# Odd gelu blocks of layer 0 turned by transposing DMAs into a table of half rows; the expert bias as a product, outputs copied by ScalarE

## The chip, the core and the metric

The kernel runs on one core of one Trainium2 chip. A core has a matmul engine (TensorE; the profile splits it into PE, the products, and PEld, the loading of their stationary operand), VectorE (DVE), ScalarE (ACT), GpSimd (POOL) and SyncE (SP, which here only issues transfers), and 16 DMA engines that carry out transfers issued from the engines' queues. SBUF is the on-chip memory of 128 partitions, PSUM the memory that products are written to. The metric is the device time of one execution in microseconds; lower is better.

## The reference, cut to what matters

Two layers work on 128 graphs of 64 nodes, N = 8192 tokens of 256 numbers, all in f32. Each layer is a graph convolution followed by a mixture of experts. The change touches the mixture of layer 0 only:

```python
H = gelu(xf @ W1 + b1)                      # 8192 x 1024, the same for all experts
probs = softmax(H @ Wg + bg)                # 8 experts
assign = argmax(probs)
for e in range(8):
    y = H @ Wd[e] + bd[e]                   # 1024 -> 256
    out += where(assign == e, probs[:, e:e+1] * y, 0)
```

Here xf is the layer-normed output of the graph convolution. Every token needs the second product with one expert's Wd alone, so the kernel sorts the rows of H by expert and runs 128 rows of one expert at a time. Layer 1 (an attention over the same graphs, and a mixture gated by a graph of 1,048,576 edges) comes behind; its edge list is sorted into keys early, beside layer 0.

## The kernel before, in words

The program is written as Python generators ("streams") whose steps are interleaved, and a scheduler then sets each engine's order. Each engine runs its instructions in that order, and each engine's DMA issues stand in its queue with the waits that they carry.

**Parts, up to about 620 us.** The 64 tiles of 128 tokens form 16 groups g of GR = 4 tiles. Parts i = 0 to 9 each take two groups of two kinds of work: `graph(g)`, the graph convolution (parts 0 to 7, L626 to L690), and `gated(g)`, the mixture's first half (parts 2 to 9, two parts behind). Beside them run `factors` (the layer norms' factors), `look` (degrees; its copies L596 run on POOL), and `collect` (parts 1 to 7): this loads a chunk of edges on SP (`src`, `dst`, L279), finds the largest keys by repeated max and match_replace on DVE, and stores what is left over with SP (`left`, L316). In parts 8 and 9 a stream of counts runs in `collect`'s place (compares on DVE L203, products L341).

`gated(g)` works in this order:
- the four tiles normed by ACT (L734), turned by TensorE (L746), copied by ACT into `zT` (L747);
- `hidden` (L489 to L503): for each of NH = 8 blocks q of 128 hidden units, two products of 128x128 by 128x512 (L498) and a gelu on ACT into `hTs[q]` (L501), a tile with hidden units on partitions and the group's 512 tokens along it. The pool `bh` has 10 such buffers;
- `turned(q)` (L752 to L756) turns block q back: four TensorE transposes of f32 128x128 (L755) into a PSUM bank of `psb` (2 buffers, shared with L746), then an ACT copy (L756) into `rows`, one buffer of 128 x 4 x 1024. It follows BEHIND = 4 blocks behind `hidden`, the last four behind the gating steps;
- gate products (L765), logits turned (L774), softmax and argmax on DVE (L779 to L794), the rank of each token among its expert's by products with a triangular matrix (L802, L803), and from it the row `pos` in the sorted table (L806 to L814);
- four indirect DMAs issued by POOL (L818), each of which sends 128 rows of 4 KB to rows `pos` of the DRAM table `hrows`.

Transfers behind these on SP: zero fills of `hrows` (from L976) and of `yrows` (L983), and, after part 7, the load of all eight Wd into `wd` (L1010).

**Early tiles, about 620 to 664 us.** `early_slots` (L871 to L943) does 8 tiles that are known to be complete two parts before the end. Its row and expert numbers are loaded into SP's and PE's registers; each tile is loaded by two transfers (L900), turned (L911, L913), multiplied by its expert (L932), gets the bias from a broadcast load (L929) by a DVE add (L940), and is stored (L942). `slot_tables` (L1012) works out beside it which 128 rows of `hrows` each of the remaining slots takes, its expert and its output row.

**Slots, about 664 to 964 us.** `slots` (L1199 to L1277) runs 60 slots, one expert each:
- `load(t)` on SP two slots ahead: `hin`, 128 rows of 4 KB (L1238), from a row number in a register; every fourth slot loads registers for the next four;
- `turn(t)` one slot ahead: eight TensorE transposes (L1247) into two PSUM banks (`pst`, 4 buffers), two ACT copies into `hTt` (L1250);
- the bias of the slot's expert broadcast over 128 rows by SP (L1262), eight f32 products of 128x128 by 128x256 that add up in `py` (L1265; `psy`, 2 buffers), the DVE add into `y` (L1273), the store to `yrows` on SP (L1274).

Beside the slots run the counts of keys (DVE compares L203, products L341), the last steps of the key sort, and `back_first` (L1171 to L1202), which for finished tiles gathers rows of `yrows` by POOL (L1193), adds them to `x` on DVE (L1184) and takes statistics (L1185). From 964 us on layer 1 runs, which the change doesn't touch.

The order of steps in the slots loop, which decides what stands between two slots' products:

```python
for t in range(first, end):
    if t + 2 < end: load(t + 2)
    if t + 1 < end: turn(t + 1)
    ...                       # bias load, 8 products, add, store
    yield add_bd              # the count stream's products come here
```

## Time and profile before

| what | value |
|---|---|
| median of 11 runs | 1975.65 us (1972.37 to 1980.22) |
| the profiled execution | 1975.63 us; span 1973.9 us; granted clock 0.987 |
| PE / PEld / DVE / ACT / POOL busy | 94 / 67 / 69 / 48 / 23 % of the span |
| slots' products L1265 | 960 records, 217.1 us |
| slots' copies L1250 on ACT | 120, 64.3 us |
| transposes L755 in `gated` | 512, 62.3 us of weight loads |
| scatters L818 on POOL | 64, 64.6 us |

All times below are of the profiled execution. A group in the profile is one line of the kernel on one engine, with the tiles it writes and reads ("py<-wd,hTt"), its shape, the number of records, the busy time, the mean of one in ns, and the engine's idle time before them with what ended most of it. A table of stretches gives, for a window A:B in us, the window's length and the busy time of each engine in it, with the number of records, then the granted clock, the share of the 16 DMA engines in use and GB/s. Matmuls are pipelined and their ends are modelled, so a busy PE isn't PE at its peak. An f32 product stands as two records where it is 512 or 256 columns wide: the 480 products of the slots are 960 records.

### The profile page before, as it was taken

To read this page: it belongs to the slowest core of one execution; us is meant where nothing else is said; L and a number is where in the kernel's file an instruction comes from. 1 tells how busy PE (TensorE), PEld (TensorE's weight loads), DVE (VectorE), ACT (ScalarE), POOL (GpSimd) and SP (SyncE) were. 2 spreads that over 40 slices of the span, in tenths; PEclk is the share of its full clock that TensorE was granted. 3 is DMA by queue.
4 is the path that set the end of the run, shared out by engine and by line. 5 is a ranking of instruction groups with operands and counts; after the bars stand their busy time and mean duration, and the time that the engine had idled before them with its cause. 6 is when DMAs were issued, how large, how long until landed. Compare 5 with 4: busy or idle time off the path is not lost. (4 is left out here: it accounts for less than half of the span.)

```text
span 1973.9 us, 32697 instructions
## 1 busy us (share of the span) xinstructions
PE 1862.1 (94%) x10609; PEld 1323.8 (67%) x10609; DVE 1353.6 (69%) x4535; ACT 948.6 (48%) x1740; POOL 452.8 (23%) x467
## 2 busy tenths in 40 slices
PE   7888998989999999999978999999999989999999
PEld 5444545444556888888745666656676758888876
DVE  6789988873356899998498755857888543334435
ACT  4867667667664222122477676422434423334322
POOL 2010110101011011111141100015677643213223
PEclk9999999999999999999988999999999999999999
DMA  9752322323425555555314211473222359889833
GB/s 295 205 170 88 120 78 78 127 88 118 138 87 179 164 179 182 169 159 173 89 54 152 67 66 42 156 202 79 64 63 61 93 188 292 275 259 276 284 114 96
DMA packets 243552, 284.91 MB, mean 144 GB/s; under 512 B 55920, under 2 KB 195312, under 8 KB 243376
## 3 DMA queue, kind: packets, MB, share of 16 engines
q1 hardware_dynamic: 209392, 221.96, 36.3%
q0 software_dynamic: 23136, 60.48, 9.4%
q10 hardware_dynamic: 10848, 0.30, 0.3%
q8 instruction: 89, 1.46, 0.3%
q14 instruction: 87, 0.71, 0.1%
HBM read 159.40 MB, written 123.18 MB: 143 GB/s over the span
## 5 line engine op out<-in xcount | busy, mean ns | idle before, releaser
L498 PE MATMUL ph<-zT,w 128*128 128x512 f32 x512 | 247.9, 605 | 5.9 <-ACT zT L747 4.8
L1265 PE MATMUL py<-wd,hTt 128*128 x960 | 217.1, 379 | 0.9 <-ACT hTt L1250 0.9
L1265 PEld LDWEIGHTS py<-wd,hTt 128*128 128x128 f32 x960 | 177.8, 190 | 22.9 <-ACT hTt L1250 1.2
L1878 POOL DMA_INDIRECT got<-tsrc,esrc x144 | 156.5, 1087 | 156.6 <-DVE esrc L1849 77.5
L1250 ACT COPY hTt<-th 128x512 f32<-128x512 f32 x120 | 64.3, 589 | 238.5 <-PE th L1247 228.8
L1415 PE MATMUL py<-w,hT 128*128 128x256 f32 x736 | 172.3, 387 | 6.8 <-DVE td L2237 4.9
L1405 PE MATMUL ph<-zT,w 128*128 128x512 f32 x368 | 169.8, 604 | 0.0
L1415 PEld LDWEIGHTS py<-w,hT 128*128 128x128 f32 x736 | 138.1, 192 | 32.4 <-issue 8.8
L498 PEld LDWEIGHTS ph<-zT,w 128*128 128x128 f32 x512 | 91.8, 192 | 97.6 <-issue 78.8
L2363 ACT ACTIVATE hT<-ph,b1e 128x256 f32<-128x256 f32 x152 | 72.1, 474 | 176.9 <-PE ph L2359 100.5
L2359 PE MATMUL ph<-zTp,w1e 128*128 128x256 f32 x608 | 139.0, 382 | 3.9 <-DMA w1e<-in_L_ffn_W_dram 3.9
L1409 ACT ACTIVATE hT<-ph,b 128x512 f32<-128x512 f32 x92 | 63.1, 688 | 164.4 <-PE ph L1405 162.7
L818 POOL DMA_INDIRECT hrows<-rows,pos x64 | 64.6, 1009 | 337.2 <-issue 164.0
L2380 DVE TENSOR_TENSOR y<-py,b2e 128x256 f32<-128x256 f32 x76 | 32.3, 425 | 157.1 <-PE py L2372 147.0
L2372 PE MATMUL py<-w,hT 128*128 x608 | 137.5, 379 | 0.0
L2359 PEld LDWEIGHTS ph<-zTp,w1e 128*128 128x128 f32 x608 | 116.5, 192 | 20.3 <-issue 4.2
L501 ACT ACTIVATE hT<-ph,b 128x512 f32<-128x512 f32 x128 | 88.1, 688 | 80.8 <-PE ph L498 76.6
L660 PE MATMUL pre<-wd 128*128 128x512 f32 x256 | 124.1, 602 | 1.9 <-ACT wd L646 1.3
L2372 PEld LDWEIGHTS py<-w,hT 128*128 128x128 f32 x608 | 112.6, 190 | 13.8
L1405 PEld LDWEIGHTS ph<-zT,w 128*128 128x128 f32 x368 | 67.8, 191 | 68.0 <-issue 67.1
L2393 POOL DMA_INDIRECT back<-yslots,place x64 | 64.6, 1009 | 166.6 <-ACT yb L1431 49.0
L755 PEld LDWEIGHTS tz<-ident,hT 128*128 128x128 f32 x512 | 62.3, 143 | 54.5 <-issue 42.8
(499 smaller groups left out, 3872.3 us busy)
## 6 DMA issues: line engine op xcount, KB each, us to landing
hin<-hrows SPq DMA_DIRECT2D x60, 512.0 KB
w1e<-in_L_ffn_W_dram SPq DMA_DIRECT2D x38, 512.0 KB
yin<-ystore SPq DMA_DIRECT2D x24, 512.0 KB
yrows<-none SPq DMA_DIRECT2D x10, 1024.0 KB
zslots<-none SPq DMA_DIRECT2D x38, 256.0 KB
zin<-zslots SPq DMA_DIRECT2D x38, 256.0 KB
yslots<-y SPq DMA_DIRECT2D x76, 128.0 KB
ystore<-y SPq DMA_DIRECT2D x72, 128.0 KB
```

What stands on the lines that cost most here:

```text
L498: nc.tensor.matmul(ph, w1[:, c, q * P : q * P + P], zT[:, c, :], start=(c == 0), stop=(c == 1))
L501: gelus.append(S.activation(hT, ph, AF.Gelu, bias=b1[:, q : q + 1]).ins)
L660: nc.tensor.matmul(pre, xnT[:, c, n * P : n * P + P], wcat[:, c, :], start=(c == 0), stop=(c == 1),)
L818: nc.gpsimd.indirect_dma_start(hrows, bass.IndirectOffsetOnAxis(ap=pos[:, t : t + 1], axis=0), rows[:, k, :], None)
L1265: nc.tensor.matmul(py, hT[:, q, :], wd[:, bass.ds(e, 1), q, :].rearrange("p e f -> p (e f)"), start=(q == 0), stop=(q == NH - 1),)
L1405: nc.tensor.matmul(ph, w1[:, e, c, q * P : q * P + P], zT[:, c, :], start=(c == 0), stop=(c == 1))
L1415: nc.tensor.matmul(py, hTs[q][:, k * P : k * P + P], w2[:, e, q, :], start=(q == 0), stop=(q == NH1 - 1))
L1878: nc.gpsimd.indirect_dma_start(got, None, tsrc, bass.IndirectOffsetOnAxis(ap=esrc[:, b, at : at + 1], axis=0))
L2359: nc.tensor.matmul(ph, w1e[:, c, q * P : q * P + P], zT[:, c, :], start=(c == 0), stop=(c == 1))
L2363: pace[:] = [S, S.activation(hT, ph, AF.Gelu, bias=b1e[:, q : q + 1]).ins]
L2372: nc.tensor.matmul(py, hTs[q][:, k * P : k * P + P], w2[:, e, q, :].rearrange("p e f -> p (e f)"), start=(q == 0), stop=(q == NH1 - 1),)
L2393: nc.gpsimd.indirect_dma_start(got[n], None, yslots[h], bass.IndirectOffsetOnAxis(ap=place[h][:, j, t : t + 1], axis=0))
```

## The change

**Tables.** `hrows` gets half its width: 512 numbers, the even blocks q. The odd blocks go into a new DRAM table `halves` with two rows of 512 sixteen-bit words for each token. Both tables are zero-filled in part 1.

**`gated(g)`.** After the gelu of an odd block, SP issues a transposing DMA that reads `hTs[q]` as 128 x 1024 sixteen-bit words and writes eight 128x128 blocks of them turned into `half_rows` (128 x 8 x 512 words, one buffer): 256 KB each, 4 per group, 64 in all. `turned` is called for the even blocks alone, 4 times per group: behind gelu 3, 5 and 7 and behind the gate products. POOL's four scatters send rows of 2 KB instead of 4 KB, and eight more scatters per group send the rows of 1 KB of `half_rows` to `halves`. Their row numbers come from `p2`, two f32 products per group with `spread_pos`, two 0/1 matrices kept in buffers that are used later for `cnt`, `row_y`, `slot_e` and `slot_row`, and one DVE instruction that makes 2 * row + (0 or 1). The four columns of row positions that `p2` multiplies are those that DVE had copied to `pos` (the tile `m`).

**Early tiles.** Each loads one 256 KB tile from `hrows`, and a second by a transposing DMA from `halves`, which arrives turned; four TensorE transposes and one ACT copy per tile stay. The bias add stays on DVE.

**Slots.** `hin` is half as wide (256 KB); `hB` arrives turned by a transposing DMA from 256 rows of `halves`, issued by SP behind `hin`. Four transposes and one ACT copy stay of eight and two. The bias comes from a bf16 product of 128x96 by 96x256 ahead of the eight f32 products: each f32 bias is split into three bf16 pieces that add up to it exactly, and a 0/1 matrix picks the expert's. `bias_tables` builds both, in three steps ahead of `slot_tables`, in the region of `w1`. The broadcast load and the DVE add are gone; ACT copies `py` to `y` and stores it from its own queue. PE alone loads the expert's number, ACT the output row's. `psy` gets 3 buffers (2 before), `pst` 3 (4 before). The gathers of `back_first` are no longer declared apart from the stores.

The diff, cut to its core:

```diff
+hrows = dram.tile([E0 * N, FD // 2], F32, name="hrows")
+halves = dram.tile([E0 * N * 2, FD // 2], U16, name="halves")
 yrows = dram.tile([(NSLOT + EARLY) * P, D], F32, name="yrows")
 psel = const.tile([P, NT], F32, name="psel")
-row_y = const.tile([P, NT], I32, name="row_y")
 off = const.tile([P, NT, 64], U8, name="off")
-cnt = const.tile([P, NT], F32, name="cnt")
+sums = const.tile([P, 2 * NT], F32, name="cnt")
+cnt, row_y = sums[:, 0:NT], sums[:, NT:].bitcast(I32)
...
+    slot_at = w0.tile([P, 2 * NSLOT], F32, name="slot_e")
+    slot_e, slot_row = (slot_at[:, i : i + NSLOT].bitcast(I32) for i in (0, NSLOT))
+    spread_pos = sums, slot_at[:, 0:P]
+    for h, to in zip(HALVES, spread_pos):
+        V.tensor_copy(
+            to.rearrange("p (n e) -> p n e", e=2), ident[:, h].unsqueeze(2).to_broadcast([P, 64, 2])
+        )
...
+            of_row = bg1.tile([P, 2], I32, name="of_row")
+            nc.gpsimd.iota(of_row[:, 0:1], pattern=[[0, 1]], base=0, channel_multiplier=1)
+            V.tensor_scalar(of_row[:, 1:2], of_row[:, 0:1], 1, None, ALU.bitwise_and)
+            odd = of_row[:, 1:2].bitcast(F32)
+            V.tensor_copy(odd, of_row[:, 1:2])
+            of_row = of_row[:, 0:1]
...
-                rows = b2.tile([P, GR, FD], F32, name="rows")
+                rows = b2.tile([P, GR, FD // 2], F32, name="rows")
+                half_rows = b2.tile([P, 2 * GR, FD // 2], U16, name="half_rows")
 
                 def turned(q):
                     th = psb.tile([P, GR * P], F32, name="tz")
                     for k in range(GR):
                         nc.tensor.transpose(th[:, k * P : k * P + P], hTs[q][:, k * P : k * P + P], ident)
-                    S.copy(rows[:, :, q * P : q * P + P], th.rearrange("p (k n) -> p k n", k=GR))
+                    at = q // 2 * P
+                    S.copy(rows[:, :, at : at + P], th.rearrange("p (k n) -> p k n", k=GR))
 
                 for q, _ in enumerate(hidden(zT, hTs)):
-                    if q >= BEHIND:
-                        turned(q - BEHIND)
+                    if q % 2:
+                        at = q // 2 * P
+                        nc.sync.dma_start_transpose(half_rows[:, :, at : at + P], hTs[q].bitcast(U16))
+                        if q > 1:
+                            turned(q - 3)
...
-                turned(NH - BEHIND)
+                turned(NH - 2)
...
-                turned(NH - BEHIND + 1)
...
-                turned(NH - BEHIND + 2)
...
-                turned(NH - BEHIND + 3)
...
+                p2 = psg0.tile([P, GR * P], F32, name="ms")[:, 0 : 2 * GR].rearrange("p (k h) -> p k h", h=2)
+                for j in range(2):
+                    nc.tensor.matmul(p2[:, :, j], spread_pos[j], m, start=True, stop=True)
...
+                at = pr.rearrange("p k e -> p (k e)")[:, 0 : 2 * GR].bitcast(I32)
+                V.tensor_scalar(at, p2.rearrange("p k h -> p (k h)"), 2.0, odd, ALU.mult, ALU.add)
+                for j in range(2 * GR):
+                    alone(
+                        nc.gpsimd.indirect_dma_start(
+                            halves, bass.IndirectOffsetOnAxis(ap=at[:, j : j + 1], axis=0), half_rows[:, j, :], None
+                        ),
+                        half_sends,
+                    )
...
-                    loaded[t] = []
-                    for i in range(0, FD, GR * P):
-                        h = bh.tile([P, GR * P], F32, name="hT")
-                        got = nc.sync.dma_start(h, hrows[bass.ds(rows_at[t], P), i : i + GR * P])
-                        for other in sends[-PART * GR :]:
-                            tc.declare_no_dep(got.ins, other, reason="rows of an early tile were sent before")
-                        loaded[t].append(h)
+                    h = bh.tile([P, GR * P], F32, name="hT")
+                    got = nc.sync.dma_start(h, hrows[bass.ds(rows_at[t], P), :])
+                    for other in sends[-PART * GR :]:
+                        tc.declare_no_dep(got.ins, other, reason="rows of an early tile were sent before")
+                    hB = bh.tile([P, GR * P], F32, name="hT")
+                    got = nc.sync.dma_start_transpose(
+                        hB.bitcast(U16).rearrange("p (q r) -> p q r", q=GR),
+                        halves[bass.ds(rows_at[t] * 2, 2 * P), :],
+                    )
+                    for other in half_sends[-PART * GR * 2 :]:
+                        tc.declare_no_dep(got.ins, other, reason="rows of an early tile were sent before")
+                    loaded[t] = h, hB
 
                 def turn(t):
 
-                    turned_[t] = []
-                    for h in loaded.pop(t):
-                        th = psb.tile([P, GR * P], F32, name="tz")
-                        for k in range(GR):
-                            nc.tensor.transpose(th[:, k * P : k * P + P], h[:, k * P : k * P + P], ident)
-                        hT = bh.tile([P, GR * P], F32, name="hT")
-                        S.copy(hT, th)
-                        turned_[t].append(hT)
+                    h, hB = loaded.pop(t)
+                    th = psb.tile([P, GR * P], F32, name="tz")
+                    for k in range(GR):
+                        nc.tensor.transpose(th[:, k * P : k * P + P], h[:, k * P : k * P + P], ident)
+                    hA = bh.tile([P, GR * P], F32, name="hT")
+                    S.copy(hA, th)
+                    turned_[t] = hA, hB
...
+                                none.unsqueeze(1).to_broadcast([P, FD // 2 // P, P]),
+                            )
+                            nc.sync.dma_start(
+                                halves[2 * e * N : 2 * (e * N + P), :].rearrange(
+                                    "(p r) (k f) -> p (r k) f", r=2, f=2 * P
+                                ),
+                                none.bitcast(U16).unsqueeze(1).to_broadcast([P, FD // 2 // P, 2 * P]),
                             )
...
+            def bias_tables():
+
+                flat1 = w1.rearrange("p c f -> p (c f)")[0:96, :]
+                at = 896
+                by_e = flat1[:, at : at + 512].bitcast(BF16).rearrange("p (e n) -> p e n", e=E0)
+                pieces = flat1[:, at + 512 : at + 640].bitcast(BF16)
+                b = flat1[:, at + 640 : at + 896]
+                r = flat1[:, at + 896 : at + 1152]
+                V.memset(b, 0.0)
+                V.tensor_copy(by_e, sel[0:96, :].unsqueeze(2).to_broadcast([96, E0, P]))
+                for i in range(3):
+                    nc.sync.dma_start(b[32 * i : 32 * i + E0, :], f0_bd)
+                yield
+                V.tensor_copy(pieces, b)
+                for i in (1, 2):
+                    V.tensor_tensor(r, b, pieces, ALU.subtract)
+                    for j in range(i, 3):
+                        rows = slice(32 * j, 32 * j + 32)
+                        V.tensor_copy(b[rows, :], r[rows, :])
+                        V.tensor_copy(pieces[rows, :], b[rows, :])
+                    yield
+                biases["by_e"], biases["pieces"] = by_e, pieces
+
+            biases = {}
+            tables = chain(bias_tables(), slot_tables())
...
-                    apart(got, stores[t + E0 :])
...
-                    h = loaded[t] = bz.tile([P, FD], F32, name="hin")
+                    h = bz.tile([P, FD // 2], F32, name="hin")
                     nc.sync.dma_start(h, hrows[bass.ds(found[t][0], P), :])
+                    hB = bz.tile([P, NH // 2, P], F32, name="hB")
+                    nc.sync.dma_start_transpose(
+                        hB.rearrange("p q r -> p (q r)").bitcast(U16).rearrange("p (q r) -> p q r", q=NH // 2),
+                        halves[bass.ds(found[t][0] * 2, 2 * P), :],
+                    )
+                    loaded[t] = h, hB
 
                 def turn(t):
 
-                    h = loaded.pop(t)
-                    hT = turned[t] = bt.tile([P, NH, P], F32, name="hTt")
-                    for i in range(0, NH, GR):
-                        th = pst.tile([P, GR * P], F32, name="th")
-                        for k in range(GR):
-                            nc.tensor.transpose(
-                                th[:, k * P : k * P + P], h[:, (i + k) * P : (i + k) * P + P], ident
-                            )
-                        S.copy(hT[:, i : i + GR, :].rearrange("p q n -> p (q n)"), th)
+                    h, hB = loaded.pop(t)
+                    hA = bt.tile([P, NH // 2, P], F32, name="hA")
+                    th = pst.tile([P, GR * P], F32, name="th")
+                    for k in range(GR):
+                        nc.tensor.transpose(th[:, k * P : k * P + P], h[:, k * P : k * P + P], ident)
+                    S.copy(hA.rearrange("p q n -> p (q n)"), th)
+                    turned[t] = hA, hB
 
                 for t in range(first, min(first + 2, end)):
                     load(t)
...
                     if t + 1 < end:
                         turn(t + 1)
                     (_, e, to), hT = found.pop(t), turned.pop(t)
-                    bd = bs.tile([P, D], F32, name="bd")
-                    nc.sync.dma_start(bd, f0_bd[bass.ds(e, 1), :].to_broadcast([P, D]))
                     py = psy.tile([P, D], F32, name="py")
+                    nc.tensor.matmul(
+                        py,
+                        biases["by_e"][:, bass.ds(e, 1), :].rearrange("p e n -> p (e n)"),
+                        biases["pieces"],
+                        start=True,
+                        stop=False,
+                    )
                     for q in range(NH):
                         nc.tensor.matmul(
                             py,
-                            hT[:, q, :],
+                            hT[q % 2][:, q // 2, :],
                             wd[:, bass.ds(e, 1), q, :].rearrange("p e f -> p (e f)"),
-                            start=(q == 0),
+                            start=False,
                             stop=(q == NH - 1),
                         )
                     y = bs.tile([P, D], F32, name="y")
-                    add_bd = V.tensor_tensor(y, py, bd, ALU.add).ins
-                    stored = nc.sync.dma_start(yrows[bass.ds(to, P), :], y)
+                    made_y = S.copy(y, py).ins
+                    stored = nc.scalar.dma_start(yrows[bass.ds(to, P), :], y)
                     apart(stored, stores + gathers)
                     stores.append(stored.ins)
-                    yield add_bd
+                    yield made_y
```

## The prediction

> **What bounds the kernel now.** I read the busy shares by slice first, then the table of stretches for the stages that the change touches, the costliest groups, the timeline of one slot, the waits of the gated parts and the transfers.
>
> The table of stretches (window; its length; PE, PEld, DVE, ACT and POOL busy; clock; DMA share; GB/s):
>
> ```profile
> 78.00:480.00 402.00, 364.81 (x1532) 196.24 (x1532) 331.58 (x1245) 283.40 (x485) 45.03 (x52) 0.98 0.35 114
> 480.00:620.00 140.00, 131.24 (x819) 74.30 (x819) 62.45 (x246) 89.38 (x146) 20.84 (x20) 1.00 0.35 125
> 664.00:964.00 300.00, 296.00 (x2581) 265.06 (x2580) 267.33 (x671) 64.81 (x122) 38.96 (x24) 1.00 0.52 166
> 800.00:850.00 50.00, 48.09 (x427) 43.19 (x426) 47.84 (x130) 10.74 (x20) 8.46 (x5) 1.00 0.52 167
> ```
>
> The slots (664 to 964) belong to PE, 296 of 300 us, with DVE close behind; ACT is idle for 235 us and the DMA engines are half used. Parts 2 to 7 of the gated work (78 to 480) are shared: PE 91%, DVE 82%, ACT 70%. In parts 8 and 9 (480 to 620) PE has 94%, and DVE is free.
>
> One slot on the timeline (start, length, engine, line):
>
> ```profile
> 822.75 0.74 PEld L341 LDWEIGHTS <-one 128*128 128x128 bf16 x16
> 822.97 0.65 PE L341 MATMUL cnt_ps<-one,one 128*128 128x64 bf16 x16
> 823.42 0.86 PEld L1247 LDWEIGHTS th<-ident,hin 128*128 128x128 f32 x8
> ...
> 824.36 3.62 PE L1265 MATMUL py<-wd,hTt 128*128 x16
> ```
>
> Nothing lies between counts, eight transposes (0.86 us, 0.1075 each) and products; the period here is 4.63 us, on the mean of the stage 300/60 = 5.0. The groups confirm it: products wait 0.9 us in all, ACT's copies 239 us.
>
> ```profile
> L1265 PE MATMUL py<-wd,hTt 128*128 x960 | 217.1, 379 | 0.9 <-ACT hTt L1250 0.9
> L1250 ACT COPY hTt<-th 128x512 f32<-128x512 f32 x120 | 64.3, 589 | 238.5 <-PE th L1247 228.8
> L818 POOL DMA_INDIRECT hrows<-rows,pos x64 | 64.6, 1009 | 337.2 <-issue 164.0
> L755 PEld LDWEIGHTS tz<-ident,hT 128*128 128x128 f32 x512 | 62.3, 143 | 54.5 <-issue 42.8
> ```
>
> The waits in the window 78 to 480 (who, for whom, total, times, longest) show where parts 2 to 7 lose time: small waits of PE and ACT on each other, and two on transfers.
>
> ```profile
> PEld tz L746 <- ACT rows L756: 21.1, 20, 2.8
> ...
> DVE key L283 <- DMA left<-key: 13.2, 8, 3.3
> ...
> ACT rows L756 <- DMA hrows<-rows,pos: 8.7, 3, 4.4
> ```
>
> **Slots, part by part.** Four transposes go: 4 x 0.1075 = 0.43 us of PE. The bias product comes: one bf16 record of 256 columns, between a bf16 record of 64 columns (0.65/16 = 0.04 us, L341) and an f32 record of the same width (217.1/960 = 0.23, L1265); I take the middle, 0.13. Net -0.30 a slot, ends -0.39 and -0.20: 60 slots give -18 us (-23 to -12). All of it is on PE, which is the path. The DVE add (0.417 x 60 = 25 us) leaves DVE, whose share would fall from 267 in 300 to 242 in 282; between 800 and 850, where DVE is as full as PE, this is what lets PE's gain through, so I add nothing for it. ACT loses 60 copies of 0.59 and gets 60 copies of 128x256 out of PSUM (0.46, from L668) and 60 store issues (0.35, from SP's L1274): 65 us becomes 78 in 282, no bound. A copy of y stands ahead of the next-but-one slot's `hA` on ACT; it ends 0.8 us after the products, and `hA` is wanted 4 us later. The bias load (0.33 of SP) goes, which was late three times for 4.2 us of DVE in all and for no PE time. `psy` with 3 buffers and `pst` with 3, now one per slot, are no tighter. Registers: PE loads one set instead of sharing two; nothing.
>
> The transposing DMA in each slot is the unknown. No row shows one. Below: 256 KB at the stage's own rate; 166 GB/s at share 0.52 is 319 GB/s at full use, 0.82 us. Above: if it moves in pieces of 16 x 2 bytes, 8192 of them at the cheapest packet in the profile (queue q10: 0.3% x 1973.9 us x 16 engines / 10848 = 8.7 ns) over 16 engines, 4.45 us. In rows of 256 bytes, 1024 packets at q1's mean of 0.363 x 1973.9 x 16 / 209392 = 54.8 ns over 16 engines give 3.5 us.
>
> ```profile
> q1 hardware_dynamic: 209392, 221.96, 36.3%
> q0 software_dynamic: 23136, 60.48, 9.4%
> q10 hardware_dynamic: 10848, 0.30, 0.3%
> ```
>
> Per slot the remaining transfers use 0.52 x 5.0 = 2.6 us of all engines, less 0.82 for the half of `hin` and about 0.4 for the bias rows: 1.4. A period of 4.7 leaves 3.3 for the transposing DMA, issued two slots ahead. I take 1 to 3 us, hidden, because these are moves of whole rows and the nearest rows are those of `hin`; the point above which it decides is 3.3.
>
> The Trainium skill bears on this in two ways. "DMA: Bandwidth & Descriptors", under Latency and other measured facts, gives an effective 261 GB/s for transposing DMAs; an estimate by it is 1.0 us, hidden. "VectorE: DVE Perf Modes", The three transpose paths, speaks against the change: 1309 ns for a 128x128 block of sixteen bits by DMA against 390 ns by TensorE, and use TensorE where PSUM will do; if the eight blocks ran in series, an estimate by it is 10.5 us per slot, more than twice the period, and the slots would grow by over 300 us. No trace here shows either, and the second disagrees with this kernel's own row for a TensorE transpose, 0.1075 us of f32.
>
> **Parts 2 to 7, 12 groups.** Sixteen of 32 transposes go: 16 x 0.107 (L755 side by side: 7 loads in 0.75 us) = -1.72. `p2` comes: nearest row L774, 8 records in 1.06; 4 records, +0.5. Net -1.2 of PE per group. ACT loses 4 copies of 0.59 = 2.4, and with them part of the L746 waits (21.1 us of weight loads over 12 groups). POOL's eight more scatters cost 1.27 each (their spacing in the trace): 10 us more per group of 36, on an engine with 45 busy of 402; behind them stand `look`'s copies, 15 us later, which are needed a part later. SP issues four more transfers, 0.33 each by L1238, at most 2.9 by the 1 MB zero fills (L983): 1.3 to 12 us per 36, on an engine that waits.
>
> The added wait: the transposing DMA of block 1 in group g+1 waits until all eight half scatters of g have landed. T being the first scatter, the twelfth goes at T + 14 and lands 3.8 to 4.6 later: T + 18 to 19.5. Block 1 of the next group is ready some 8 us after the next group's start, and T repeats every 36 us, with its gelus mostly behind T + 0 to + 9:
>
> ```profile
> 547.43 1.08 POOL L818 DMA_INDIRECT hrows<-rows,pos  x1 [18.94 <-issue]
> 548.82 0.96 POOL L818 DMA_INDIRECT hrows<-rows,pos  x1 [0.30 <-issue]
> ...
> 555.53 1.07 ACT L756 COPY rows<-tz 128x512 f32<-128x512 f32 x2
> ```
>
> So SP is held for 10 to 15 us per group. Queued behind it on SP: `left` stores and `src`/`dst` loads of `collect` (DVE waits for the former already, 13.2 us in 8 times), the zero fills, and the Wd loads. By the order of instructions, few of these stand behind such a wait (the `left` stores of three chunks clearly, of two more slightly); each costs DVE 3 to 5 us, and DVE has 18% to spare. I take -0.85 per group: -10 us for the twelve. The ends: -30 if ACT's and the waits' relief all comes through (2.5 per group), +25 if DVE stands for 3 us more in each of the groups beyond its slack.
>
> **Parts 8 and 9, 4 groups** of 25.1 us: -1.2 of PE each, -5. Against it: the first copy into `rows` now follows gelu 4 (T + 5) instead of 5 (T + 7), and it needs the four scatters of `hrows` landed (T + 3.8 + 3.8 = T + 7.6 to 8.4): ACT waits 2 to 3 us where it waited 0 to 0.7. With PE's gelu buffers full that shows as 1 to 2 us per group. Sum 0, ends -6 and +8.
>
> **Early tiles.** 8 x 0.43 = -3.4 of transposes. SP comes free for the early register loads only when group 15's four transposing DMAs are issued: the last scatters of group 14 go at 597.9, its half rows are free at about 617, and four issues of 0.33 to 2.9 follow: 619 to 629, where the first early load went at 613 to 616 and the first product at 621.8. +4, up to +14. Sum +1. The bias tables add about a dozen DVE instructions, beside counts: nothing, +2 if not.
>
> Sum: -18 - 10 + 0 + 1 = -27. The profiled execution took 1975.63 and its median is 1975.65, so 1948.6; I say 1949.
>
> **Rivals.**
> R1, slower: a transposing DMA takes longer than 3.3 us of all engines, and the slots run at DMA's pace. At the upper end of 4.45: 4.45 + 1.4 = 5.85 instead of 4.97 per slot, +53; in parts 8 and 9 `half_rows` is free at T + 19, four times 4.45 end at T + 37, and the next half scatters are due at about T + 30, so some 5 us slip in each of four groups, +20. With -10 elsewhere about 2038; worse if the blocks run in series. For it: nothing shows the price, and a two-byte layout suggests small pieces. Against it: the DMA engines stand idle for 48% of the stage.
> R2, slower: the wait on `half_rows` on SP holds up `collect`. It decides from about 2.5 us of lost DVE time per group on; at 5 us for 12 groups, +60 - 10 - 18: about 2008. For it: DVE is at 46 of 50 in some stretches, and its waits on `left` are there already. Against it: few transfers stand behind.
> R3, faster: DVE alone sets parts 2 to 7, whose PE gain is lost; the slots alone gain: 1975 - 18 + 3 = 1960.
> R4, no change within 0.2% (4 us, about what a measurement of this kernel can tell): gains of the slots eaten by stalls before them, 1975.
>
> **How the numbers follow.** The forecast -27 gets 0.40, R3 0.17, R4 0.06, R1 0.17, R2 0.20. Faster 0.57, same 0.06, slower 0.37. The first two together span 1928 to 1968 (slots -23 to -12, gated -30 to 0, early to +5), with the forecast at 1949. The range has to take in most of R1 and R2: 1928 to 2038 leaves out a tenth above (blocks in series) and a twentieth below.
>
> **What the profile after would show.** Right: slots with a period of 4.6 to 4.7 and PE still 97% full; L341, four weight loads of 0.43 together, one bf16 record near 0.13, products 3.62; the transposing DMA landing in under 5 us, the DMA share at or below 0.7; DVE 25 us less busy between 664 and 945; groups at 35 us in parts 2 to 7, with SP waiting on the half scatters and DVE's wait on `left` near 13 us. Wrong by R1: products waiting on `hB`, DMA share above 0.9. Wrong by R2: `key` on DVE waiting for `left` or `src` by 40 us or more. Also wrong: a first early product after 630.

## The result and the profile after

The changed kernel takes 2023.42 us (median of 8 runs, 2022.36 to 2025.24) where the kernel before took 1975.78 (31 runs): a ratio of 1.0241, interval 1.0232 to 1.0249. It is slower by 2.4%; the forecast was 1949 us, faster by 1.3%. The profiled execution has a span of 2020.4 us, 46.5 more than before.

The table of stretches of the kernel after, in the columns explained above:

```profile
78.00:480.00 402.00, 335.46 (x1307) 177.57 (x1306) 327.97 (x1243) 251.46 (x415) 117.18 (x123) 0.92 0.51 136
480.00:620.00 140.00, 130.66 (x723) 68.71 (x722) 57.84 (x234) 82.77 (x135) 56.31 (x58) 0.99 0.53 148
664.00:964.00 300.00, 277.37 (x2318) 242.99 (x2317) 257.20 (x704) 52.97 (x109) 40.31 (x35) 0.97 0.60 151
```

PE is busy for 29 us less in the first window and for 19 less in the third (where the early tiles now reach into it), and the kernel did not get shorter: PE now waits, and its work comes later. Where the 46.5 us arise is read from fixed points on the two timelines:

| point on the timeline | before | after | behind by |
|---|---|---|---|
| first scatter of group 0 | 127.92 | 124.48 | -3.4 |
| of group 3 | 236.06 | 244.49 | 8.4 |
| of group 12 (the first of parts 8 and 9) | 547.43 | 572.00 | 24.6 |
| of group 14 (inside parts 8, 9) | 597.90 | 621.55 | 23.7 |
| first product of an early tile | 621.8 | 653.4 | 31.6 |
| first f32 product of the slots | 663.8 | 700.7 | 36.9 |
| last slot's output out of PSUM | 962.5 | 1002.0 | 39.4 |
| layer 1's first transposes | 963.5 | 1006.5 | 43.1 |
| end of the span | 1973.9 | 2020.4 | 46.5 |

Half of the loss is made in parts 2 to 7 and eight us at the early tiles; the slots, which were to gain 18, gain nothing, and some 7 us go between the last slot and the end.

**Parts 2 to 7.** Waits of the kernel after in the window 78 to 480 (who, for whom; total, times, longest):

```profile
DVE key L284 <- DMA left<-key: 50.1, 11, 9.6
...
PE tz L651 <- ACT zT L757: 38.8, 5, 11.4
ACT pr L795 <- DVE pr L794: 24.2, 5, 6.6
...
PE tz L756 <- ACT zT L757: 15.9, 5, 8.1
```

Before, these were 13.2 us for `left`, 0.5 for `pr`, and for the first of the two on `zT`:

```profile
PE tz L645 <- ACT zT L747: 8.9, 10, 2.3
```

The second, ahead of `z`'s transposes, stood on ACT's copies into `rows` instead (PE 15.4 us); that wait is gone, as the prediction hoped, and the ones on `zT` outweigh it. One of the five places, line by line of the timeline (start, length, engine, line, what; in brackets the idle time before and its cause):

```profile
214.19 0.82 DVE L316 TENSOR_REDUCE rest<-key 128x1 f32<-128x640 f32 x1
...
217.41 4.00 SPq L773 DMA_TRANSPOSE half_rows<-hT  x3
...
221.46 0.58 SPq L317 DMA_DIRECT2D left<-key  x1
...
223.64 1.04 PE L756 MATMUL tz<-ident,z 128*128 128x128 f32 x8
...
225.54 1.06 ACT L693 ACTIVATE wd<-wd 128x1024 f32<-128x1024 f32 x1
...
226.10 0.43 DVE L284 TENSOR_SCALAR key<-src 128x512 f32<-128x512 int32 x1 [9.59 <-DMA left<-key]
...
231.91 0.17 DVE L793 TENSOR_REDUCE m<-ms 128x4 f32<-128x32 f32 x1
...
232.87 0.23 ACT L795 ACTIVATE pr<-pr 128x32 f32<-128x32 f32 x1 [6.27 <-DVE pr L794]
...
234.41 1.15 ACT L694 ACTIVATE wd<-wd,ones_col 128x1024 f32<-128x1024 f32 x1
...
235.47 1.05 ACT L757 COPY zT<-tz 128x512 f32<-128x512 f32 x2
...
236.09 1.11 PE L651 MATMUL tz<-ident,wd 128*128 128x128 f32 x4 [11.40 <-ACT zT L757]
```

Four queues in a row pass the delay on. On SP the store of `left` stands behind three transposing DMAs, which wait for the half scatters of the group before and then hold SP for 1.33 us each. DVE, which needs the `key` buffer that this store reads, stands still for 9.6 us, and the softmax's maximum (L793) stands behind it, though the last product that it reads ended at 223.3. ACT waits for the softmax before its exponential (L795). And behind that exponential and the graph convolution's logarithm (L694) stand both copies of `zT`, whose transposes ended at 224.7. PE has nothing to do for 11.4 us.

The last link is new. In the kernel before, ACT's order in each group but the first was: softmax's exponential, the graph's exponential, one `zT` copy, the logarithm, the other copy. One such group of the kernel before:

```profile
226.14 0.23 ACT L781 ACTIVATE pr<-pr 128x32 f32<-128x32 f32 x1
...
227.48 1.08 ACT L687 ACTIVATE wd<-wd 128x1024 f32<-128x1024 f32 x1
228.44 0.60 ACT L747 COPY zT<-tz 128x512 f32<-128x512 f32 x1
...
230.35 1.15 ACT L688 ACTIVATE wd<-wd,ones_col 128x1024 f32<-128x1024 f32 x1
231.41 0.56 ACT L747 COPY zT<-tz 128x512 f32<-128x512 f32 x1
```

After, in every second group, it is: the graph's exponential, softmax's exponential, logarithm, both copies. The five waits of PE that end at L651 are in those groups.

Idle PE costs a second time. The same place in rows of 5 us (PE and PEld are the first two busy times, the clock is the third figure from the end):

```profile
220.00:225.00 5.00, 4.68 (x40) 2.96 (x31) 0.00 (x0) 2.66 (x6) 0.00 (x0) 1.00 1.32 199
225.00:230.00 5.00, 0.00 (x0) 0.00 (x0) 3.73 (x8) 1.58 (x2) 0.00 (x0) 0.77 0.14 28
230.00:235.00 5.00, 0.00 (x0) 0.00 (x0) 4.97 (x22) 2.10 (x3) 0.00 (x0) 0.50 0.34 105
235.00:240.00 5.00, 3.47 (x8) 1.90 (x9) 5.00 (x23) 3.58 (x5) 0.00 (x0) 0.50 0.00 0
240.00:245.00 5.00, 5.00 (x21) 2.71 (x20) 5.00 (x32) 2.49 (x4) 0.51 (x1) 0.86 0.00 0
```

The granted clock falls to 0.50 while PE is idle (from 224.7 on) and stays there for some 5 us of its next work (PE starts again at 236.1; 0.86 as the mean of 240 to 245 puts the end at about 241.4). The group of `hidden`'s products shows the sum: 633 ns against 605 before, 512 records, 14 us. The Trainium skill has the rule, in "TensorE: Matmul & The Clock Gate" (Part 1: The HAM clock gate): the clock halves after an idle stretch of about 3.4 us and comes back after as long a busy one. The trace is near the first (0.77 as the mean of 225 to 230 puts the fall at about 227.7, 3.0 us after the last product) and takes more for the second, about 5.3 us; the prediction priced none of it.

**Early tiles.** SP's queue on the timeline:

```profile
639.34 5.42 SPq L773 DMA_TRANSPOSE half_rows<-hT  x4
...
646.43 0.40 SPq L924 DMA_DIRECT2D hT<-hrows  x1
```

Group 15's four transposing DMAs stand ahead of the first load of an early tile, which went at 613 before. PE waits 11.7 us for that load.

**Slots.** One slot on the timeline:

```profile
804.10 1.25 SPq L1299 DMA_TRANSPOSE hB<-halves  x1
804.10 0.37 ACT L1341 COPY y<-py 128x256 f32<-128x256 f32 x1 [2.98 <-PE py L1333]
...
804.35 0.42 PEld L1311 LDWEIGHTS th<-ident,hin 128*128 128x128 f32 x4
...
804.74 0.10 PEld L1325 LDWEIGHTS <-w 96*128 x1
804.85 0.27 PE L1325 MATMUL py<-w 96*128 96x256 bf16 x1
...
808.62 0.37 ACT L1341 COPY y<-py 128x256 f32<-128x256 f32 x1 [2.98 <-PE py L1333]
```

The period is 4.52 us, and nothing waits for the transposing DMA. But the mean over the 59 periods is 5.00 (from 706.78 to 1001.95), as it was before (4.97). Some slots take 5 to 7 us, with two waits (window 664 to 1002):

```profile
DVE x L1244 <- DMA yearly<-yrows,cnt: 37.1, 13, 5.2
...
PE cnt_ps L342 <- DVE one L204: 16.2, 13, 3.4
```

Before, there was no wait of the first kind, and the second stood at 3.0 us:

```profile
PE cnt_ps L341 <- DVE one L203: 3.0, 3, 1.9
```

**Into layer 1.** ACT's first work of layer 1, first after the change and then before:

```profile
1005.88 2.57 ACT L1441 ACTIVATE z<-x,fac 128x256 f32<-128x256 f32 x5 [3.56 <-SPq L1397]
```

```profile
962.68 2.57 ACT L1373 ACTIVATE z<-x,fac 128x256 f32<-128x256 f32 x5 [6.36 <-PEq L1329]
```

It starts 3.9 us after the last slot's output (L1341, at 1001.95) instead of 0.1, and the profile puts the wait down to SP's queue. PE stands for 4.6 us and then works at a clock of 0.52 from 1008 to 1013 (1.00 from 965 to 970 before). What SP still has to do there isn't shown.

### The profile page after: what moved, and what is told of

Its sections match the earlier page's. It is cut to its first block, busy times and chain, and to the rows that moved or that the text cites. A ratio compares the mean times of both kernels' runs of the same rounds, so it can differ in the third digit from the quotient of the medians.

```text
span 2020.4 us, 32276 instructions
## 1 busy us (share of the span) xinstructions
PE 1844.1 (91%) x10205; PEld 1299.5 (64%) x10205; DVE 1339.2 (66%) x4506; ACT 907.8 (45%) x1668; POOL 574.2 (28%) x595
## 5 line engine op out<-in xcount | busy, mean ns | idle before, releaser
L504 PE MATMUL ph<-zT,w 128*128 128x512 f32 x512 | 262.8, 633 | 9.2 <-ACT hT L507 6.0
L1473 PE MATMUL ph<-zT,w 128*128 128x512 f32 x368 | 168.1, 599 | 0.0
L1333 PE MATMUL py<-wd,hA 128*128 x480 | 146.2, 387 | 0.0
L1333 PE MATMUL py<-wd,hB 128*128 x480 | 145.8, 386 | 0.0
L843 POOL DMA_INDIRECT halves<-half_rows,pr x128 | 129.6, 1012 | 39.0 <-issue 32.3
L1341 ACT COPY y<-py 128x256 f32<-128x256 f32 x60 | 22.4, 373 | 183.4 <-PE py L1333 175.5
```

The source lines that it names most:

```text
L504: nc.tensor.matmul(ph, w1[:, c, q * P : q * P + P], zT[:, c, :], start=(c == 0), stop=(c == 1))
L843: nc.gpsimd.indirect_dma_start(halves, bass.IndirectOffsetOnAxis(ap=at[:, j : j + 1], axis=0), half_rows[:, j, :], None),
L1333: nc.tensor.matmul(py, hT[q % 2][:, q // 2, :], wd[:, bass.ds(e, 1), q, :].rearrange("p e f -> p (e f)"), start=False, stop=(q == NH - 1),)
L1473: nc.tensor.matmul(ph, w1[:, e, c, q * P : q * P + P], zT[:, c, :], start=(c == 0), stop=(c == 1))
```

## The experiments

Sixteen of the eighteen runs below were on chips where the kernel before took 2005 to 2013 us in the median; the extra time lies in layer 1, which the change doesn't touch. The last two and the result ran where it took 1976. Ratios are to the kernel before on the same chip in the same set of runs, and times on the timeline are compared between like chips.

### The transposing DMAs late, the gather's add late, both; the bias part alone

e1_late issues the four transposing DMAs of a group together, after the last gelu:

```diff
                         if q % 2:
-                            at = q // 2 * P
-                            nc.sync.dma_start_transpose(half_rows[:, :, at : at + P], hTs[q].bitcast(U16))
                             if q > 1:
                                 turned(q - 3)
+                        if q == NH - 1:
+                            for o in range(1, NH, 2):
+                                at = o // 2 * P
+                                nc.sync.dma_start_transpose(half_rows[:, :, at : at + P], hTs[o].bitcast(U16))
```

> Against the changed kernel (2023.4 us). Theory A: SP, which works in order, is held at the transposing DMA of block 1 until the half scatters of the group before have landed (223 us in 35 waits), and the `left` stores behind it make DVE wait (50.1 us in 11 times, 13.2 in 8 before); softmax, ACT and PE follow. With all four transposing DMAs issued behind the last gelu, the half rows are free when SP comes to them: DVE waits for `left` under 20 us, the first product of the early tiles 12 to 25 us earlier, time 1998 to 2011. Rival B: it is the twelve scatters of POOL, or the transposing DMAs themselves, that hold the groups up: the wait moves elsewhere and the time stays within 4 us of 2023 or grows.

e2_late_add gives the gathered rows three buffers and adds them one tile later; e3_both is the two together:

```diff
-name="be", bufs=2
+name="be", bufs=3
...
-                        t, y = held.pop()
+                        t, y = held.pop(0)
...
-                        if held:
+                        if len(held) > 1:
                             add()
```

> Against the changed kernel (2023.4 us). Theory C: in the slots each gather now waits for the newest store of ACT, so the rows land late for DVE's add (37.1 us in 13 waits, none before), the compares behind it are late and PE waits for them (16.2 us, 3.0 before). With the add one tile later (three buffers for two), DVE's wait falls under 8 us and PE's under 6, slots 10 to 15 us shorter, time 2008 to 2014. Rival D: DVE has too much work between 700 and 850 us, and the wait is only where it shows: time within 4 us of 2023.

> Both edits. If A and C hold and are apart, their gains add: 1985 to 2000. If one of them hides the other, no better than the better of the two.

e4_bias is the kernel before with only the bias product, ACT's outputs and the gathers that are no longer declared apart:

```diff
+                        nc.tensor.matmul(py, biases["by_e"][...], biases["pieces"], start=True, stop=False)
...
-                        add_bd = V.tensor_tensor(y, py, bd, ALU.add).ins
-                        stored = nc.sync.dma_start(yrows[bass.ds(to, P), :], y)
+                        made_y = S.copy(y, py).ins
+                        stored = nc.scalar.dma_start(yrows[bass.ds(to, P), :], y)
...
-                        yield add_bd
+                        yield made_y
```

> Against the kernel before (1975.7 us): only the bias as a bf16 product and the outputs by ACT, with the gathers no longer apart; tables, transposes and loads as before. Theory C: 60 products of about 0.11 us of PE (+7) and DVE's wait for late gathers (+10 or so, of which the removed adds pay part): 1980 to 1993, with DVE waiting over 20 us for gathers. The prediction's view (DVE's relief pays, gathers cost nothing): 1970 to 1984 with no such wait.

Measured: 1.0440 [1.0387, 1.0493] for e1, 1.0422 [1.0378, 1.0466] for e2, 1.0431 [1.0392, 1.0469] for e3, and 1.0158 [1.0118, 1.0198] for e4. The changed kernel itself came to 1.0413 [1.0375, 1.0451] on such a chip (e0_after, below). So moving the issues together gained nothing: DVE still waits 31.5 us for `left` (34.0 in e0_after). Why isn't shown; one reason may be that four issues in a row hold SP for over 5 us at one time instead of at several. e2 gained nothing either, and says little: in the order that the scheduler made, an add still stands right behind its own gather (issued at 909.83, added at 913.48 after a wait of 5.5 us), and DVE's wait for the gather stayed at 37.1. The surprise is e4: the part for which I had named a bare 0.13 us per slot makes the kernel 1.6% slower by itself. Its slots take 324 us (664 to 988), with PE waiting for counts 15.7 us.

### A second key tile; ordered gathers; both

e0_after is the changed kernel once more. e5_two_keys lets odd chunks use another `key` tile, so that DVE needn't wait for the store of the chunk before:

```diff
-            keys = self.work.tile([P, CHUNK + PER], F32, name="key")
+            keys = self.other if c % 2 else self.work.tile([P, CHUNK + PER], F32, name="key")
```

e6_gather declares the gathers apart from the stores of other tiles again, and makes each wait for the last slot that writes its rows:

```diff
                         gathers.append(got.ins)
+                        apart(got, stores[t + E0 :])
+                        for other in stores[t + E0 - 1 if t else 0 : t + E0]:
+                            tc.add_manual_dep(got.ins, other.name, ...)
```

e7_keys_gather is the two together.

> The changed kernel itself once more, beside the next three on the same chip, so that they can be compared with it: ratio to the kernel before near 1.024 on an undisturbed chip; on the chip of the first four runs, where the kernel before took 2007 us, near 1.04.

> Against the changed kernel on this chip. The key tile gets a second buffer (in room that the Wd region leaves free), so DVE no longer waits for the `left` store that SP issues late. Theory A: that wait is what the groups lose in parts 2 to 7: DVE's waits for `left` fall under 10 us, the first scatter of group 14 comes 15 to 25 us earlier, and the time falls by 15 to 25 us. Rival A2: SP is late for the src and dst loads as well, and the wait only changes its name: under 6 us gained. Rival B: the transposing DMAs or POOL's twelve scatters hold the groups: no change.

> Against the changed kernel on this chip. Each gather waits only for the stores that hold its rows, as before the change, and no longer for the newest one. Theory C: DVE's wait for gathered rows falls from 37 us under 8, PE's for counts from 16 to under 6, the slots get 8 to 14 us shorter. Rival D (DVE has too much other work there): within 3 us.

> Both edits. By A and C 25 to 38 us less than the changed kernel, about the time of the kernel before plus 10 to 20 us, what is left being the early tiles' late start (some 10 to 15 us).

Measured: e5 1.0317 [1.0280, 1.0354], e6 1.0356 [1.0324, 1.0388], e7 1.0281 [1.0250, 1.0313], against 1.0413 for e0. The second key tile is worth 17.6 us: the first scatter of group 14 comes at 629.5 instead of 644.2. So DVE's wait on `left` does reach the end. It isn't the whole: DVE's wait falls from 34.0 to 5.8 us and ACT's for `pr` from 18.5 to 10.4, but PE still waits 31.4 us in five times for `zT` (34.8 in e0_after), since ACT's order is as it was. In e6 DVE's wait for the gather is gone (2.1 us of 35.8), but its slots take 299.5 us by the first and last f32 products (300.1 in e0_after), and PE's wait for the counts is as long as before:

```profile
DVE one L204 <- PE cnt_ps L342: 34.0, 15, 2.7
...
PE cnt_ps L342 <- DVE one L204: 16.0, 11, 2.9
```

The theory that the gather made the slots slow falls: DVE's wait only changed its partner. Both engines wait for each other at the counts, which means that these stand in the wrong order.

### The kernel before once more; the slots paced

The loop around the slots runs each step of the counts, of the key sort and of `back_first` under `with tc.issue_after(last)`, where `last` is what the slot yielded. Before, that was DVE's bias add; after, it is ACT's copy. So nothing holds DVE's order to the slots any longer, and the key sort's steps run ahead of the counts. The stretches of the kernel after show it (DVE is the third busy time):

```profile
700.00:750.00 50.00, 49.55 (x406) 43.66 (x406) 49.08 (x111) 9.85 (x21) 1.30 (x1) 0.94 0.65 159
...
850.00:900.00 50.00, 47.22 (x420) 41.69 (x419) 36.66 (x85) 9.56 (x21) 5.74 (x5) 1.00 0.59 150
```

DVE is full at first and has too little to do later. e8_paced restores the tie by a DVE copy of one column:

```diff
-                        made_y = S.copy(y, py).ins
+                        S.copy(y, py)
...
-                        yield made_y
+                        tick = bs.tile([P, 1], F32, name="tick")
+                        yield V.tensor_copy(tick, py[:, 0:1]).ins
```

e9_paced_gather adds e6's edit, e10_all the edits of e5 and e6. b0_before is the kernel before, for its stages on this chip.

> The kernel before, profiled on a chip of this group: where the chips of the last two calls are slower than the one of the first profile (2008 against 1976 us) by code loads, its profile shows waits put down to an unknown queue, about 30 us of them, most in layer 1, and the parts, early tiles and slots within 5 us of the first profile.

> The changed kernel with one DVE copy of 128x1 from `py` per slot, which the loop yields in place of ACT's copy, so that DVE's counts, key steps and gather adds are queued behind a slot's end again, as behind the bias add before. Against the changed kernel (ratio 1.041 to the kernel before on such a chip). Theory E: what the slots lost is this order: without it the key steps run ahead (DVE 48 of 50 us busy between 700 and 850, 34 after), and PE waits for counts. Then the slots take 280 to 290 us instead of 299, PE waits for counts under 6 us, ratio 1.032 to 1.037. Rival C: the gathers' wait for the newest store does it: slots stay at 296 or more, DVE still waits 20 us or more for gathered rows. Rival D: too much DVE work in all: no change.

> As the last, and each gather waits only for the stores that hold its rows. By E alone: within 3 us of the last run. If C adds to it: another 5 to 12 us less, slots 272 to 282 us.

> As the last, with two key tiles: the three repairs together. By A and E: 17 us (two keys) and 10 to 25 us (slots) below the changed kernel, ratio 1.018 to 1.027. What is left above 1 is then the late start of the early tiles and ACT's waits for `rows` and for buffers.

Measured: in b0 the parts, early tiles and slots stand within 5 us of the first profile, as expected, and the other 31 us of its later end lie in layer 1, but only 19 us of waits are put down to an unknown queue; what makes those chips slower isn't shown. e8 1.0311 [1.0257, 1.0364], e9 1.0332 [1.0276, 1.0388], e10 1.0203 [1.0151, 1.0255]. The slots of the changed kernel once more, and of e8:

```profile
733.00:1032.00 299.00, 282.15 (x2400) 248.57 (x2399) 247.04 (x611) 56.54 (x118) 31.14 (x24) 0.98 0.59 143
```

```profile
739.00:1025.00 286.00, 280.16 (x2402) 247.62 (x2402) 251.86 (x669) 56.51 (x118) 30.61 (x24) 0.99 0.64 149
```

The same work takes 13 us less; PE waits for counts 5.7 us instead of 16.6, and for the gather DVE waits 0.2. Ordering the gathers by hand adds nothing to it (e9).

### The bias part paced; what the transposing DMAs cost

e4b_bias_paced is e4 with the DVE tick. e11_free_halves sends a constant tile in the half scatters instead of `half_rows`, so that no transposing DMA waits for a scatter (e11 and e12 leave the odd blocks' values out of the result). e12_plain is e11 with plain DMAs in place of the 64 transposing ones. e13_twice adds to each slot a second transposing DMA into a tile that nobody reads:

```diff
-                                halves, bass.IndirectOffsetOnAxis(ap=at[:, j : j + 1], axis=0), half_rows[:, j, :], None
+                                halves, bass.IndirectOffsetOnAxis(ap=at[:, j : j + 1], axis=0), off[:, 0:16, :]..., None
...
-                            nc.sync.dma_start_transpose(half_rows[:, :, at : at + P], hTs[q].bitcast(U16))
+                            nc.sync.dma_start(half_rows[:, :, at : at + P], hTs[q].bitcast(U16)...)
...
+                        hC = bz.tile([P, NH // 2, P], F32, name="hC")
+                        nc.sync.dma_start_transpose(hC..., halves[bass.ds(found[t][0] * 2, 2 * P), :])
```

> The kernel before with the bias product and ACT's outputs alone, and the DVE copy of 128x1 per slot that keeps DVE's order. Without that copy this part alone cost 1.58% (slots 324 us against 299). Theory E: 1.000 to 1.006, slots 298 to 308 us. If it is the gathers' wait for the newest store or the product's own 0.11 us that cost the 25 us: 1.010 or more.

> The changed kernel, with the eight half scatters of each group sending a constant tile in place of `half_rows` (so the odd blocks' values are left out of the result); all transfers are still issued, but no transposing DMA waits for a scatter. Theory A to the end: that wait is what the gated parts and the early tiles lose. Against the changed kernel (ratio 1.041 on such a chip): `left` waits under 10 us, the early tiles' first product 25 to 40 us earlier, ratio 1.020 to 1.028. If two key tiles had already taken all that there is to take (17 us): 1.031 to 1.035.

> As the last, with a plain DMA of the same bytes in place of each of the 64 transposing DMAs of the gated parts. If the transposing itself costs something there (SP is held 1.33 us per issue against 0.33, and the pieces are small), 4 to 12 us less than the last run; if not, within 4 us.

> The changed kernel, with a second transposing DMA of the same rows in each slot, into a tile that nothing reads. By the prediction's middle (1 to 3 us of all engines, hidden): the slots stay within 4 us of 299 us, and the DMA share of the slots tells the price by its rise. By rival R1 (4.45 us): two of them and the rest take 10 us a slot, the slots grow by 200 us or more.

Measured: e4b 1.0034 [1.0014, 1.0054], e11 1.0341 [1.0307, 1.0376], e12 1.0321 [1.0265, 1.0378], e13 1.0627 [1.0591, 1.0663].

With the tie restored, the bias part alone costs 0.3% instead of 1.6%, and its slots 303 us instead of 324:

```profile
664.00:988.00 324.00, 307.70 (x2637) 274.51 (x2636) 252.91 (x627) 86.63 (x179) 28.88 (x25) 0.98 0.41 131
```

```profile
663.00:966.00 303.00, 301.81 (x2635) 270.07 (x2635) 255.12 (x680) 85.86 (x178) 30.27 (x24) 1.00 0.43 139
```

Without the waits on half scatters (e11) DVE's wait on `left` is 18.8 us instead of 34.0 and the first scatter of group 14 comes at 638.7 instead of 644.2; the early tiles' first product comes 10.0 us sooner (664.4 for 674.4), where 25 to 40 were expected. So the wait on half scatters is a small part of the loss in parts 2 to 7: PE still waits 32.9 us for `zT` at the copies that stand behind the exponential (34.8 in e0_after). With plain DMAs as well (e12) group 14 comes at 633.3, and the early tiles' first product stands 23.8 us behind it, no later than in the kernel before (b0 24.5; e11 25.7, e0_after 30.2). The intervals of e11 and e12 overlap, so whether the transposing itself costs something there stays open. In the slots a second transposing DMA does show:

```profile
739.00:1081.00 342.00, 297.42 (x2394) 258.61 (x2394) 246.86 (x602) 55.61 (x118) 26.77 (x24) 0.94 0.82 171
```

The DMA engines are busy for 0.82 x 342 = 280 us instead of 0.59 x 299 = 176: 1.7 us of all 16 engines for one transposing DMA of 256 KB, as the engines' busy time counts it. No instruction waits for the one per slot in the changed kernel; a second one is not hidden: the slots take 43 us more, with waits of ACT and PE for the loads.

### The order of the softmax and the graph's steps

With two key tiles and paced slots (e10) the first scatter of group 14 still came 26 us late (624.5 against 598.0 in b0), and PE waited 30.4 us for `zT` in five times. Two hints on the order, on top of e10. e14_gate_first issues the key rounds on DVE after the softmax maximum recorded last; e15_exp_first has in addition:

```diff
+                    with tc.issue_after(exps[-1]) if exps else ExitStack():
-                    S.activation(sp, sp, AF.Exp, scale=-1.0)
-                    S.activation(sp, sp, AF.Ln, bias=ones_col)
+                        S.activation(sp, sp, AF.Exp, scale=-1.0)
+                        S.activation(sp, sp, AF.Ln, bias=ones_col)
```

where `exps` holds the softmax's exponentials. ACT's order then has one or both `zT` copies ahead of the graph's exponential or logarithm in every group, as before the change.

> The version with two key tiles, ordered gathers and paced slots, plus one hint: the key rounds that are recorded after a group's first softmax step on DVE (the maximum m) are issued after it. In that version parts 2 to 7 still end 26 us later than in the kernel before, and PE waits 30.4 us in 5 times for ACT's zT copies (8.9 before). On the trace around 302 to 310 us, m is ready on PE at 301.9, stands on DVE behind key rounds until 305.7, ACT's exp waits 2.2 us for it, and zT, whose transposes ended at 303.3, stands on ACT behind the exp and the logarithm until 309.9. Theory D (DVE's order is what makes the softmax late): ACT's wait for pr falls from 9.4 to under 4 us, PE's for zT from 30 to about 20, the first scatter of group 14 from 624.5 to about 615, ratio 1.015. Theory E (ACT's own order, the exp and zT behind the two steps of the graph convolution, is enough by itself): PE's wait for zT stays within 5 us of 30, and the ratio within 0.3% of 1.020.

> The same, plus a second hint: the exponential and the logarithm of the graph convolution on ACT are issued after the last softmax exponential recorded, which gives ACT nearly the order it had in the kernel before (softmax's exponential, one zT copy, the graph's exponential, the logarithm, the other zT copy). If what is left of the loss in parts 2 to 7 is this order (theories D and E together): PE's wait for zT falls to 8 to 15 us, the first scatter of group 14 to about 603 to 608 (598 in the kernel before on such a chip), the slots end some 14 us sooner than they would have by the paced slots, and the ratio is 1.008 to 1.012. If what is left is something else (rows waiting for scatters, the half scatters' traffic): the wait falls but the first scatter of group 14 stays above 618, ratio 1.017 or more.

Measured: e14 1.0153 [1.0136, 1.0170] with group 14 at 621.5; e15 1.0056 [1.0039, 1.0073] with group 14 at 601.4, 3.5 us behind the kernel before instead of 23.7. The waits in 78 to 480, of e14 and then of e15:

```profile
PE tz L654 <- ACT zT L760: 56.3, 5, 13.7
...
ACT pr L798 <- DVE pr L797: 30.7, 5, 8.6
...
DVE key L306 <- DMA left<-key: 20.9, 3, 9.9
```

```profile
ACT pr L799 <- DVE pr L798: 30.8, 5, 9.0
...
PE tz L661 <- ACT wd L655: 26.3, 5, 8.1
...
DVE key L306 <- DMA left<-key: 21.0, 3, 10.1
...
PE tz L654 <- ACT zT L761: 1.2, 5, 0.2
```

This pair is the clearest of all. DVE still stands 10 us for `left`, ACT still waits 31 us for DVE's softmax, and PE's wait of 56 us for `zT` is down to 1.2, because the copies that it needs no longer stand behind the late exponential. The delay isn't gone: PE now stands five times at L661, 26.3 us in all, for ACT's `wd` (L655), which stands behind the same exponential. At 231.5 that wait is 4.9 us; before it PE has 4.5 us of products that it can do. Waits for `zT` and `wd` together fall from 68 to 39 us. 19.1 us of the kernel's time come back by the order of two ACT instructions. The hint on DVE alone did not do what I expected: the waits for `pr` grew from 9.4 to 30.7 us, probably since the key rounds that it pushes back make the next `left` late (DVE waits for it 39.0 us, 5.1 in e10). Group 14 then stands where the changed kernel itself has it, with one key tile and no hint (621.6).

The clock follows: `hidden`'s products take 622 ns in e14 and 606 in e15, as before the change (605).

No version beats the kernel before. The best with the tables of half rows, e15, is 0.56% slower; the bias part alone, paced (e4b), 0.34%.

## Why the prediction was wrong

The time lies in the range, 1928 to 2038, and on the wrong side: I gave 0.57 to faster and 0.37 to slower. Point by point:

**Parts 2 to 7: -10 forecast, +24.6 measured. This step failed most.** "ACT loses 4 copies of 0.59 = 2.4, and with them part of the L746 waits" counted instructions that go and did not look at the order of those that stay. The relief came (PE's 15.4 us for `rows` ahead of those transposes are gone), but the waits for `zT` grew from 12 to 56 us. Three of the four copies behind the gating steps are gone, and the scheduler put both `zT` copies behind the graph's exponential, the softmax's and the logarithm in every second group; that the one made the other is argued, not shown. "Each costs DVE 3 to 5 us, and DVE has 18% to spare" was the other half: DVE's waits were up to 9.6 us, and the slack of a mean doesn't help the softmax, which stands on DVE right behind the waiting instruction. R2 had this mechanism in its name (`left` on SP, 40 us or more on DVE as its mark, 50.1 seen), at 0.20 and at 5 us per group; it lacked the link by which DVE's delay reaches PE, and the half clock behind each long wait of PE, some 14 us in `hidden`'s products. Cutting either link helps and neither cut is complete: the wait on `left` by e5 (17.6 us, with 31.4 us of PE's waits left), the order on ACT by e15 (19.1 us less than e14, with 26.3 left at another copy).

**Slots: -18 forecast, about +2 measured by the mean of a period.** The arithmetic of the slot was right, though the period of the slot that it shows, 4.63, was misread. The products behind those at 824.36 are

```profile
829.20 3.62 PE L1265 MATMUL py<-wd,hTt 128*128 x16
```

so that slot, with 16 count products, took 4.84. With eight transposes and the bias product (e4b) the usual period is 4.96, after the change 4.52: 0.32 less than the 4.84 before, against 0.30 in the working; the bias product's record is 0.27 us long but only 0.11 lies between its neighbours' weight loads, near the 0.13 taken. What failed is "so I add nothing for it" of the DVE add that goes. The add was also what tied DVE's order to the slots. With a tick in its place the mean period is 4.76 and the slots gain 12 to 15 us (from the first output to the last: e8 280.8 against 295.6 in b0, e15 280.7 against 293.1 before). R3 and R4 both counted on slots that gain by their arithmetic alone, and fall with this step.

**Parts 8 and 9: 0 forecast, -0.9 measured** (group 12 to group 14: 50.5 before, 49.6 after). Right, on the chip of the result.

**Early tiles: +1 forecast.** The first product stands 31.9 us behind group 14's scatter instead of 23.9: 8 us where SP's four issues were priced at "+4, up to +14". The mechanism was right, as e11 and e12 show, and the size lies between its bounds. Another 5 us go until the slots' first product. The first early product, at 653.4, stands well behind 630, which the prediction had named as a sign of being wrong.

**Into layer 1: not in the sum.** The prediction has no term for the step from the slots to layer 1, where the changed kernel loses 3.7 us, and after which it loses 3.4 more.

**The transposing DMA: hidden, 1 to 3 us forecast.** Right: 1.7 us of all engines by e13. R1, at 4.45, falls. Of the Trainium skill's two figures that the prediction quoted, "DMA: Bandwidth & Descriptors" (Latency and other measured facts) with its 261 GB/s, by estimate 1.0 us, is nearer than "VectorE: DVE Perf Modes" (The three transpose paths), whose 1309 ns per block in series would give, by estimate, 10.5; the runs say 1.7, and e13 moves one per 2.9 us (120 in 342), so they don't take 10.5 one after another. The issue holds SP for 1.25 to 1.33 us, where a plain load holds it 0.33 to 0.35; the prediction had bounds of "0.33 each ..., at most 2.9", and the measured hold lies between them. What it costs in the end is not told apart from the waits.

**What stays open.** e15 still loses 13.2 us of span: 3.5 by group 14, 7 more by the first early product (632.6 against 621.8), 6 more by the slots' first product (680.4 against 663.8), which wait for their `hin` (5.0 us) and run at half clock; the slots give 12 back; 4 go on the way into layer 1, where ACT waits 4.0 us for SP's queue, so layer 1 begins 8.8 us late; and 4 to 5 go inside it, part of them at a clock of 0.50 from 973 to 978. Why SP is late there isn't shown; the versions with transposing DMAs in the slots have that wait (e0_after 4.3, e5 4.2, e8 3.9), and e4b, which lacks them, waits 1.4 us for ACT's own queue. On the chips where the kernel before took about 2008 us, ACT and DVE of the changed kernel also waited in parts 8 and 9 for a queue that the profile doesn't name, up to 15.3 us at a time (e0_after); this isn't explained. In e10, which ran on such a chip, the effects of the repairs can't be told apart from it.

## What to carry to other kernels

Before a saving is counted, compare the order of the instructions that stay, engine by engine: an instruction that goes can have been what kept two others apart, or what an order hint was tied to. When a hint names "the last instruction of this unit" and the change moves that to another engine, the tie to the first engine is lost, and a copy of one column gives it back. A delay in an in-order queue costs what stands behind it on the next engine, not what its mean share leaves free; follow it through every queue to the one that bounds the kernel, and cut it at the cheapest link, which may be the order of two instructions at the far end. Then look where the wait went: it may stand behind the same instruction under another name.

## What the runs showed of the hardware that I had not expected

- A transposing DMA of 256 KB holds the issuing engine's queue for 1.25 us (loads from DRAM) to 1.33 us (between buffers) in the median, up to 2.8; a plain load of the same size holds it 0.33 to 0.35, a plain DMA between the same buffers 0.60 (e12).
- Its work is about 1.7 us of the 16 engines by their busy time in e13, some 154 GB/s.
- 11 us without products took PE's granted clock to 0.50, from about 3 us after the last of them, and it stayed there for some 5 us of the next.
- ACT's copy of 128x256 out of PSUM takes 0.373 us; I had taken 0.46 from an instruction with a scale.
